# A style-modulated convolution kernel: both pairs of a quad in one product, four products in one PSUM region

## The chip, the cores and the metric

The kernel runs on one core of a Trainium2 chip. The metric is the device time of one launch in microseconds (us); lower is better.

## What is computed

128 samples of 64 channels and 1024 positions go through four 1-D convolutions of three taps (same, up by two with a blur, same, blur with down by two), and the result is added to the input. Each sample has its own weights:

```python
def _layer(x, style, w, b, mw, mb, typ):
    s = style @ mw.T + mb
    weight = SCALE * w * s[:, None, :, None]
    demod = lax.rsqrt(jnp.sum(weight * weight, axis=(2, 3)) + EPS)
    weight = weight * demod[:, :, None, None]
    ...                     # convolution of this type, then + b
x = x + L0(x, cond_512, ...)    # layers 'same', 'upsample', 'same', 'downsample'
```

Nothing nonlinear lies between the layers, so away from the ends of a row the four layers are one convolution of nine taps whose weights differ by sample. The kernel computes those nine weights for each sample (64x64 matrices) and convolves once. The six columns at the ends are computed layer by layer, for all samples together.

## The kernel before

**Units.** Two samples make a *pair* `p`: one sample in partitions 0 to 63, one in 64 to 127. Two pairs make a *quad* `q`; there are 32. TensorE works as four 64x64 quadrants, two row halves by two column halves, each with its own stream, so four matmuls run side by side. All data are fp32, and each fp32 matmul of the program is two records of LDWEIGHTS and MATMUL in the trace.

**Weights.** Stages 1 to 3 (`stage1` L362, `stage2` L393, `stage3` L430) build a quad's nine taps by matmuls into PSUM units `psS`, `psR`, `psW`; ScalarE evicts each with a scale per sample (`scaled_copy` L340) into `wd`, `S`, `R`, `Wf`. `stage3` runs in two parts. `combine` (L468 to L473, with `residual` L460) makes three sums of taps, the tile `H`, on VectorE. One PSUM buffer serves all these units in turn, `psE` of the ends too.

**Convolution.** The nine taps are done as three triples, in a scheme that needs five products instead of nine: each product is three matmuls over shifted columns. The input row lies in three interleaved planes. For a pair, `pre1` and `pre2` turn the planes `X` into five inputs, the five slots of a tile `T`, by way of a tile `G`: `G` by VectorE (L499, L504), slots 2 and 3 by GpSimd (`rest`, L510 and L511; for the first pairs VectorE), slot 4 by VectorE (L522), slots 0 and 1 by VectorE (L532). `SLOT` says which product reads which slot: products 0 and 4 read slots 0 and 1, products 1, 2 and 3 read slots 2, 3 and 4. `product` (L550) issues 12 matmuls of 170 columns; the two column halves of TensorE hold the two halves of a row's columns. `convA12` and `convA3` put products 1, 2 and 3 into three regions of one PSUM tile `psA`. ScalarE copies one of them (`copy_m1`, L573), `seed1` and `seed2` (L585) combine them on VectorE into `y1` and into two regions of the PSUM tile `Y`, and `convB` adds products 0 and 4 on top of `Y`. `output` (L642) scales and adds a bias on ScalarE, `store` (L647) sends half a pair, `load` (L132) fetches a pair.

**Order.** The order on each engine is the order of the program text (`manual_schedule`). The main loop runs over quads. In iteration q, with `c = q + 2` and `s = q + 3`, TensorE does: stage 2 of c, convB of the quad's first pair, stage 3 part 0 of c, products 1 and 2 of the next quad's first pair, stage 3 part 1, product 3, convB of the second pair, stage 1 of s, products 1 to 3 of the next quad's second pair. In some iterations `slot` adds a matmul group for the ends (`psE`, L792) and `extra` adds VectorE work for them. A prologue prepares quads 0 to 2.

**Buffers.** Tiles come from pools; a pool holds `bufs` buffers for each tag. Waits between engines are set by the framework from who writes and reads which tile. Before, `T` has four buffers of one pair each, and pair p+4 takes that of pair p: `pre1(p + 4)` stands behind `convB(p)` in the text.

## Time and profile before

| | |
|---|---|
| device time, three runs | 496.41, 496.79, 497.35 us (median 496.79) |
| the profiled execution | span 494.6 us; its own device time is not listed apart, the median lies 2.2 us above the span |
| instructions in the span | 28356 |
| GpSimd | busy 137.9 us (28%) |
| DMA | 70.81 MB, mean 143 GB/s |
| TensorE's granted clock, mean over the span | 0.998 |

The span runs from the first to the last instruction of the core. An engine's busy time says how much of the span it worked, not whether the work set the end. The chain follows the end back: at each step to what released an instruction, or to the one before it on the engine. In the tables of groups, a row is a line, engine and operation, `out<-in`, shapes, and a count; behind the bar stand busy us and mean ns of one. Matmul records are the latency of one and overlap.

### The profile page before, as it was taken

How to read it: one execution, taken by the hardware profiler on the slowest of the kernel's cores; microseconds unless marked ns; L12 is line 12 of the kernel's file. 1: busy time of each engine (PE TensorE's matmuls, PEld its weight loads, DVE VectorE, ACT ScalarE, POOL GpSimd, SP SyncE). 2: the span in 40 equal slices, each digit the busy share in tenths (PEclk: the TensorE clock that was granted, in tenths of full speed). 3: DMA queues.
4: the chain of work that ended last, by engine and by line, in shares of the span. 5: the costliest groups of instructions: out<-in, count | busy, mean ns of one | idle time of the engine just before them, and what ended most of it. 6: DMA issues, size and time to landing. Idle time of an engine off the chain costs nothing.

```text
span 494.6 us, 28356 instructions
## 1 busy us (share of the span) xinstructions
PE 485.9 (98%) x12600; PEld 475.6 (96%) x12600; DVE 442.4 (89%) x926; ACT 325.3 (66%) x797; POOL 137.9 (28%) x198
## 2 busy tenths in 40 slices
PE   8999999999999999999999999999999999999995
PEld 6899999999999999999999999999999999999995
DVE  5898989999999989988889998879999989988995
ACT  5566766766866657757667767657667667767652
POOL 3253234353322212212212222212222212222210
PEclk9999999999999999999999999999999999999999
DMA  8132654335544425553535554425544436544323
GB/s 255 50 98 89 216 168 150 108 115 174 173 157 148 153 67 175 173 173 115 139 99 173 168 165 147 144 76 173 163 147 155 135 99 191 173 160 130 97 109 129
DMA packets 37610, 70.81 MB, mean 143 GB/s; under 512 B 4208, under 2 KB 29040, under 8 KB 37488
## 3 DMA queue, kind: packets, MB, share of 16 engines
q1 hardware_dynamic: 37408, 68.88, 44.4%
q8 instruction: 99, 1.62, 1.4%
q14 instruction: 23, 0.19, 0.1%
q10 hardware_dynamic: 80, 0.11, 0.1%
HBM read 35.36 MB, written 33.62 MB: 139 GB/s over the span
## 4 chain that ended last, share of the span: by engine, by line
PE 96%; ACT 2%; DVE 1%; issue 0%; ACTq 0%; DVEq 0%
PE psA L550 32%; PE Y L550 22%; PE psR L393 17%; PE psW L430 14%; PE psS L362 7%; PE psE L792 2%; PE Y L173 1%; PE Y L316 1%; ACT Wf L340 0%; ACT m L573 0%; ACT R L340 0%; ACT ssq L206 0%; ACT sc L206 0%; PE psM L192 0%; DVE Y L585 0%
## 5 line engine op out<-in xcount | busy, mean ns | idle before, releaser
L550 PE MATMUL psA<-T,H 64*64 64x170 f32 x4608 | 205.4, 304 | 0.6 <-ACT m L573 0.6
L550 PEld LDWEIGHTS psA<-T,H 64*64 64x64 f32 x4608 | 188.4, 133 | 1.4 <-POOL o L644 0.9
L510 POOL TENSOR_TENSOR T<-G 128x342 f32<-128x342 f32 x62 | 57.9, 934 | 317.6 <-DVE G L504 194.8
L550 PE MATMUL Y<-T,Wf 64*64 64x170 f32 x3072 | 139.8, 304 | 1.4 <-ACT m L573 1.4
L550 PEld LDWEIGHTS Y<-T,Wf 64*64 64x64 f32 x3072 | 127.2, 133 | 2.6 <-ACT m L573 2.0
L642 ACT ACTIVATE o<-Y,oc,dm 128x340 f32<-128x340 f32 x125 | 79.5, 636 | 56.4 <-PE Y L550 56.1
L430 PE MATMUL psW<-R,par 64*64 64x256 f32 (+3 forms) x1536 | 98.7, 349 | 0.0
L393 PE MATMUL psR<-S,E 64*64 64x192 f32 (+1 forms) x2304 | 93.3, 299 | 0.1
L585 DVE SCALAR_TENSOR_TENSOR Y<-psA,u 128x340 f32<-128x340 f32 (+1 forms) x132 | 66.4, 507 | 30.1 <-ACT o L642 27.7
L340 ACT ACTIVATE Wf<-psW,t 128x256 f32<-128x256 f32 (+1 forms) x252 | 75.3, 381 | 22.6 <-PE psW L430 22.2
L430 PEld LDWEIGHTS psW<-R,par 64*64 64x64 f32 x1536 | 85.4, 133 | 2.5
L393 PEld LDWEIGHTS psR<-S,E 64*64 64x64 f32 x2304 | 85.9, 133 | 0.6 <-ACT S L340 0.2
L340 ACT ACTIVATE R<-psR,tC 128x448 f32<-128x448 f32 x63 | 36.5, 630 | 57.2 <-PE psR L393 57.2
L642 ACT ACTIVATE o<-y,oc,dm 128x170 f32<-128x170 f32 x125 | 65.7, 526 | 0.0
L499 DVE SCALAR_TENSOR_TENSOR G<-X 128x688 f32<-128x688 f32 x64 | 56.0, 874 | 4.6
L511 POOL TENSOR_TENSOR T<-G 128x342 f32<-128x342 f32 x62 | 57.2, 922 | 0.0
L532 DVE TENSOR_TENSOR T<-G 128x684 f32<-128x684 f32 x64 | 55.7, 871 | 0.0
L362 PE MATMUL psS<-wd,par 64*64 64x192 f32 x768 | 44.9, 329 | 0.0
L362 PEld LDWEIGHTS psS<-wd,par 64*64 64x64 f32 x768 | 37.0, 136 | 0.7 <-ACT raw L660 0.3
L573 ACT ACTIVATE m<-psA 128x340 f32<-128x340 f32 x64 | 29.2, 456 | 9.2 <-PE psA L550 6.4
L585 DVE SCALAR_TENSOR_TENSOR y<-psA,v 128x340 f32<-128x340 f32 x64 | 32.7, 512 | 2.2
L522 DVE TENSOR_TENSOR T<-X 128x342 f32<-128x342 f32 x64 | 33.6, 524 | 0.1
(131 smaller groups left out, 388.6 us busy)
## 6 DMA issues: line engine op xcount, KB each, us to landing
out<-o SPq DMA_DIRECT2D x126, 255.0 KB, 4.3
X<-in_x SPq DMA_DIRECT2D x60, 344.0 KB, 3.5
X<-in_x SPq DMA_DIRECT2D x60, 172.0 KB, 3.2
X<-in_x SPq DMA_DIRECT2D x4, 516.0 KB, 6.4
Xe<-in_x_ends SPq DMA_DIRECT2D x1, 512.0 KB, 5.8
par<-in_params SPq DMA_DIRECT2D x2, 192.0 KB, 3.5
out<-o SPq DMA_DIRECT2D x2, 170.0 KB, 2.8
par_s<-in_params_s SPq DMA_DIRECT2D x1, 196.0 KB, 2.8
```

The lines of the kernel that those rows point to most:

```text
L340: nc_a.activation(dst, src, AF.Copy, scale=f)
L362: nc.tensor.matmul(ps[r][cols, k * C : (k + K) * C], woi[2][rows, k, :], src[rows, :], start=(k == 0), stop=(k == K - 1), skip_group_check ...
L393: nc.tensor.matmul(ps[r][cols, lo * C : (lo + m) * C], E[rows, e + 2, :], src[rows, a, :], start=(n == 0), stop=(n == 8), skip_group_check ...
L430: nc.tensor.matmul(ps[r][cols, (lo - t_lo) * C : (hi - t_lo) * C], woi[0][rows, k, :], rt[c][rows, lo - k : hi - k, :], start=(k == order[0]),
L499: nc_v.scalar_tensor_tensor(g[:, PL:], X[:, : 2 * PL], 0.5, X[:, PL:], op0=ALU.mult, op1=ALU.subtract)
L510: eng.tensor_add(t[:, 2, :NJ], plane(g, 2), plane(g, 1))
L511: eng.tensor_sub(t[:, 3, :NJ], plane(g, 2), plane(g, 1))
L522: eng.tensor_sub(t[:, 4, :NJ], plane(X, 3), plane(X, 1))
L532: nc_v.tensor_sub(t[:, 0:2, :NJ], both(a, PL), both(b, 1))
L550: nc.tensor.matmul(ps[s][cols], w, Ts[p][rows, SLOT[m], j : j + NB], start=(g == 0 and m not in (0, 4)), stop=(g == 2), skip_group_check=True,
L585: nc_v.scalar_tensor_tensor(out, x, f, y, op0=ALU.mult, op1=ALU.add)
L642: nc_a.activation(dst, src, AF.Identity, bias=add, scale=d3)
```

## The change

**Both pairs in one product.** `X`, `G`, `T`, `o` and the sums hold a quad. The two column halves of TensorE take the two pairs, not two halves of the columns, so a matmul has 340 columns and a product of a quad is 12 matmuls, where it was 24. `T` has two buffers, each of a quad; `G`, `m3` and `y1` have one. `t_tile` makes `T` and `G` of a quad at its first use, which in the loop is `in3(c)`.

**Four products in one region.** For a quad, product 3 starts a region of the PSUM tile `A`; ScalarE copies it (`copy_m3`); product 1 is added on top; VectorE reads the sum (`sum1`); product 2 is added; VectorE reads again (`sum2`: it seeds `Y` and finishes `y1`); product 0 is added on top, and the region is the output of one plane. Product 4 goes into `Y`. Constant factors move into the weights.

**Stage 3 by kind of tap.** The nine taps lie as three kinds by three groups. Part 0 does kinds 0 and 1, part 1 kind 2, each from weights scaled beforehand (`scaled_weights`, on GpSimd); there are 9 steps of 192 and 128 columns, where there were 6 of 128 to 320. An eviction is one instruction, where it was two. `combine` is split into `combine_a` and `combine_b`.

**The loop.** The order in an iteration is new, with `n = q + 1`. A quad is stored in two DMAs, where it was four. The host changes the layout of the output.

The diff, cut; lines that are removed stand only where short:

```diff
-    tpool = ctx.enter_context(tc.tile_pool(name="tpool", bufs=4))
-    mpool = ctx.enter_context(tc.tile_pool(name="mpool", bufs=2))
-    gpool = ctx.enter_context(tc.tile_pool(name="gpool", bufs=2))
-    opool = ctx.enter_context(tc.tile_pool(name="opool", bufs=4))
+    tpool = ctx.enter_context(tc.tile_pool(name="tpool", bufs=2))
+    mpool = ctx.enter_context(tc.tile_pool(name="mpool", bufs=1))
+    gpool = ctx.enter_context(tc.tile_pool(name="gpool", bufs=1))
+    opool = ctx.enter_context(tc.tile_pool(name="opool", bufs=2))
...
-    NX = 4
+    NX = 2
     PL = NXC // 3
-    Xs = [const.tile([P, NXC], F32, name=f"X{i}") for i in range(NX)]
-    def load(p, planes=slice(0, 3)):
-        if p < NP:
+    Xs = [const.tile([P, 2, NXC], F32, name=f"X{i}") for i in range(NX)]
+    def load(q, planes=slice(0, 3)):
+        if q < NQ:
             at = slice(planes.start * PL, planes.stop * PL)
-            nc.sync.dma_start(Xs[p % NX][:, at], x[p, :, at])
+            for c in range(2):
+                nc.sync.dma_start(Xs[q % NX][:, c, at], x[2 * q + c, :, at])
...
+    w0s = [woi[0]] + [const.tile([P, K, C], F32, name=f"w0s{i}") for i in range(2)]
+    idn3 = const.tile([P, C], F32, name="idn3")
+    def scaled_weights():
+        for t, f in zip(w0s[1:], (1.0 / 3.0, -2.0)):
+            nc_g.tensor_scalar_mul(t, woi[0], f)
+        nc_g.tensor_scalar_mul(idn3, idn, 1.0 / 3.0)
...
+        kinds = ((0, 1), (2,))[part]
+        n = 0
+        for i, kind in enumerate(kinds):
+            for k in range(K):
+                gs = [g for g in range(K) if 0 <= K * g + kind - k < 7]
+                lo, m = gs[0], len(gs)
+                first = K * lo + kind - k
+                n += 1
+                for r, rows in enumerate(HALF):
+                    for c, cols in enumerate(HALF):
+                        at = (K * i + lo) * C
+                        nc.tensor.matmul(
+                            ps[r][cols, at : at + m * C],
+                            w0s[kind][rows, k, :],
+                            rt[c][rows, first : first + K * (m - 1) + 1 : K, :],
+                            start=(n == 1),
+                            stop=(n == K * len(kinds)),
+                            skip_group_check=True,
+                        )
+        for r in range(2):
+            dst = W[:, r, kinds[0] : kinds[-1] + 1].rearrange("c t g o -> c (t g o)")
+            scaled_copy(engs[r], dst, ps[r][:, : len(kinds) * K * C], t0[:, q, r : r + 1])
+        return ps
...
+    def residual(q):
+        W = Wq[q][0]
+        for r in range(2):
+            v = W[:, r, 1, 1, :]
+            nc_v.scalar_tensor_tensor(v, idn3, t3[:, q, r : r + 1], v, op0=ALU.mult, op1=ALU.add)
+    def sum_of(out, x, f, y, op=ALU.add):
+        nc_v.scalar_tensor_tensor(out, x, f, y, op0=ALU.mult, op1=op)
+    def taps(q):
+        W, H_ = Wq[q]
+        return *(W[:, :, i] for i in range(K)), *(H_[:, i] for i in range(3))
+    def combine_a(q):
+        chain.pop(q)
+        a, b, c, h1, h2, h3 = taps(q)
+        sum_of(h1, c, -2.0, a)
+        residual(q)
+        sum_of(h3, h1, 1.0 / 6.0, b)
+    def combine_b(q):
+        a, b, c, h1, h2, h3 = taps(q)
+        sum_of(h2, c, -0.5, a)
+        sum_of(h1, b, -3.0, h2, ALU.subtract)
+        sum_of(h2, h2, -1.0 / 3.0, b)
...
+    NJ = NB + 2
+    Ts = {}
+    Gs = {}
+    A = {}
+    SLOT = {0: 0, 4: 1, 1: 2, 2: 3, 3: 4}
...
+    def t_tile(q):
+        if q not in Ts:
+            Ts[q] = tpool.tile([P, 2, 5, PL], F32, tag="T", name=f"T{q}")
+            Gs[q] = gpool.tile([P, 2, 3 * PL], F32, tag="G", name=f"G{q}")
+        return Xs[q % NX], Ts[q], Gs[q]
+    def in3(q, pairs=BOTH_PAIRS):
+        if q < NQ:
+            X, t, g = t_tile(q)
+            nc_v.tensor_sub(t[:, pairs, 4, :NJ], plane(X, 3, pairs), plane(X, 1, pairs))
+    def in_g01(q, c):
+        if q < NQ:
+            X, t, g = t_tile(q)
+            sum_of(g[:, c, PL:], X[:, c, : 2 * PL], 0.5, X[:, c, PL:], ALU.subtract)
+    def in_g2(q, pairs=BOTH_PAIRS):
+        if q < NQ:
+            X, t, g = t_tile(q)
+            sum_of(plane(g, 2, pairs), plane(X, 3, pairs), 0.5, plane(X, 2, pairs), ALU.subtract)
+    def in1(q, eng):
+        if q < NQ:
+            X, t, g = t_tile(q)
+            eng.tensor_add(t[:, :, 2, :NJ], plane(g, 2), plane(g, 1))
...
+    def in04(q, c):
+        if q < NQ:
+            X, t, g = t_tile(q)
+            a, b = g[:, c, :NJ], g[:, c, 2 * PL : 2 * PL + NJ]
+            both = lambda v, step: bass.AP(v.tensor, v.offset, [list(v.ap[0]), [step, 2], [1, NJ]])
+            nc_v.tensor_sub(t[:, c, 0:2, :NJ], both(a, PL), both(b, 1))
+    def product(q, m, ps, groups=range(K)):
+        W, H_ = Wq[q]
+        for g in groups:
+            for s, rows in enumerate(HALF):
                 for c, cols in enumerate(HALF):
+                    if m in (0, 4):
+                        w = W[rows, c, m // 2, g, :]
+                    else:
+                        w = H_[rows, m - 1, c, g, :]
                     nc.tensor.matmul(
+                        ps[cols, s, :NB],
+                        w,
+                        Ts[q][rows, c, SLOT[m], g : g + NB],
+                        start=(g == 0 and m == 3),
+                        stop=(g == K - 1),
                         skip_group_check=True,
                     )
...
+    def conv3(q):
+        A[q] = ps_conv.tile([P, 2, 512], F32, tag="u", name=f"psA{q}")
+        product(q, 3, A[q])
+    def copy_m3(q):
+        m3c[q] = m_tile("m3", q)
+        nc_a.copy(m3c[q], A[q][:, :, :NB])
+    def conv1(q):
+        product(q, 1, A[q])
+    def sum1(q):
+        y1w[q] = m_tile("y1", q)
+        sum_of(y1w[q], A[q][:, :, :NB], 2.0, m3c[q])
+    def conv2(q):
+        product(q, 2, A[q])
+    def sum2(q):
+        a = A[q][:, :, :NB]
+        sum_of(Y[:, :, :NB], m3c.pop(q), 3.0, a)
+        nc_v.tensor_sub(y1w[q], y1w[q], a)
+    def conv4(q):
+        product(q, 4, Y)
+    def conv0(q, *groups):
+        product(q, 0, A[q], groups)
...
+    def output(q, i, s, eng=nc_a):
+        if q not in os:
+            os[q] = opool.tile([P, 2, K, NB], F32, tag="o", name=f"o{q}")
...
+        src = (A[q][:, s, :NB], y1w[q][:, s], Y[:, s, :NB])[i]
...
+    def store(q, s, planes=slice(0, K)):
+        nc.sync.dma_start(
+            out[q, :, s, planes.start * NB : planes.stop * NB],
+            os[q][:, s, planes].rearrange("c i j -> c (i j)"),
+        )
...
     stage3(0, 0, None, BOTH)
     stage3(0, 1, ps_conv, BOTH)
     stage1(1, ps_conv)
     stage1(2)
+    combine_a(0)
+    combine_b(0)
     const_rest(0, PART[0], const_of(0, PART[0]))
+    in2(0, nc_v)
     stage2(1, ps_conv)
+    conv3(0)
+    copy_m3(0)
     const_first(1, PART[0])
+    in04(0, 0)
+    in04(0, 1)
...
+    conv1(0)
...
+    sum1(0)
...
+    stage3(1, 1)
+    mod_by_layer(LATER, raw[0][:, 0], ssq, AF.Square)
+    in_g01(1, 0)
     scale3(3)
+    conv2(0)
...
     EXTRA = {
+        (0, 0): lambda: (
+            var_inverse(PART[1]),
+            var_newton(PART[1]),
+            table_A(PART[1], dm[:, 2, PART[1]]),
+            [of(PART[1]) for of in (table_C, vector_c0, table_3, vector_Da)],
+        ),
...
+        n, c, s = q + 1, q + 2, q + 3
         if q == 1:
             nc.sync.dma_start(Xe, x_ends)
         if q == 5:
             zeros()
         if c < NQ:
             stage2(c)
+        if q == 0:
+            var_matmul(PART[1], var_of(PART[1]), start=False)
+            var_root(PART[1], var_of(PART[1]))
+        sum2(q)
+        if n == NQ - 1:
+            conv3(n)
+            copy_m3(n)
+            conv4(q)
+            for i in range(2):
+                output(q, 2, i)
+            combine_b(n)
+            in04(n, 0)
+            in04(n, 1)
+            conv1(n)
+            for i in range(2):
+                output(q, 1, i)
+            sum1(n)
+            conv0(q, 0, 1)
+            conv2(n)
+            conv0(q, 2)
+            for i, eng in enumerate(BOTH):
+                output(q, 0, i, eng)
+                store(q, i)
+            continue
+        if q == 0:
+            combine_a(1)
+        if n < NQ:
+            combine_b(n)
+        conv4(q)
+        for i in range(2):
+            output(q, 2, i)
+        if n == NQ:
+            for i, eng in enumerate(BOTH):
+                output(q, 1, i, eng)
+            for i in range(2):
+                store(q, i, slice(1, 3))
+            conv0(q, *range(K))
+            for i, eng in enumerate(BOTH):
+                output(q, 0, i, eng)
+                store(q, i, slice(0, 1))
+            break
         if c < NQ:
             stage3(c, 0)
+        conv3(n)
+        copy_m3(n)
+        if q == 0:
+            in_g01(1, 1)
+            in_g2(1)
+            load(n + NX)
+            in1(1, nc_g)
+            in2(1, nc_g)
+        in04(n, 0)
+        in04(n, 1)
+        in3(c)
         if c < NQ:
             stage3(c, 1)
+        conv0(q, 0, 1)
+        if q in SLOTS:
+            slot(*SLOTS[q])
+        conv1(n)
+        for i in range(2):
+            output(q, 1, i)
+        for i in range(2):
+            in_g01(c, i)
+        in_g2(c)
+        load(c + NX)
+        in1(c, nc_g)
+        in2(c, nc_g)
+        extra(q, 0)
+        sum1(n)
         extra(q, 1)
+        conv0(q, 2)
+        output(q, 0, 0)
         if s < NQ:
             stage1(s)
+        output(q, 0, 1)
         if s + 1 < NQ:
             scale3(s + 1)
+        conv2(n)
         if c < NQ:
+            combine_a(c)
+        for i in range(2):
+            store(q, i)
```

## The prediction

> **What bounds the kernel now.** First the page: busy shares and the chain that ended last.

> ```profile
> PE 485.9 (98%) x12600; PEld 475.6 (96%) x12600; DVE 442.4 (89%) x926; ACT 325.3 (66%) x797; POOL 137.9 (28%) x198
> ...
> PE 96%; ACT 2%; DVE 1%; issue 0%; ACTq 0%; DVEq 0%
> ```

> TensorE (PE) carries 96% of the chain. Whether it streams at its limit is read from the chain in order of time and from matmul groups by shape (columns of the chain: start us, us, what).

> ```profile
> 256.04 0.08 PE psR L393
> ...
> 268.13 2.31 PE psA L550 x64
> ...
> 270.44 0.07 PE psR L393
> ```

> ```profile
> L430 PE MATMUL psW<-R,par 64*64 64x320 f32 x256 | 30.4, 430 | 0.0
> ...
> L393 PE MATMUL psR<-S,E 64*64 64x128 f32 x1024 | 70.4, 269 | 0.0
> ```

> From 320 to 128 columns a matmul gets shorter by 161 ns: 0.839 ns a column. The 64 records of 170 columns took 2.31 us, 16 in each quadrant: 144.4 ns, of which 142.6 are columns and 2 a fixed cost. Stage 2 to stage 2 is one quad: 14.40 us. The columns of a quad per quadrant are 60 x 170 (conv), 6 x 192 (stage 1), 10 x 192 and 8 x 128 (stage 2), 2688 (stage 3): 16,984, or 14.25 us, and 96 records by 2 ns make 14.44. So PE streams without a gap, and only columns, records or a new wait can move the time. Waits on PE are few: 0.98 us at 99.0, 1.03 at 114.3, 0.90 at 480.3.

> Then what a change of buffers can do: who waited for the T tiles (waits: us in total, times, longest), and one such place in the timeline.

> ```profile
> POOL T L510 <- PE Y L550: 46.8, 10, 7.0
> ```

> ```profile
> 250.73 0.51 DVE L504 SCALAR_TENSOR_TENSOR G<-X 128x342 f32<-128x342 f32 x1
> ...
> 251.51 0.96 PE L550 MATMUL Y<-T,Wf 64*64 64x170 f32 x18
> ...
> 252.89 0.91 POOL L510 TENSOR_TENSOR T<-G 128x342 f32<-128x342 f32 x1 [5.84 <-PE Y L550]
> ```

> This is iteration 14. GpSimd writes slot 2 of T[33] into the buffer of T[29]. Slot 2 of T[29] was read by product 1, in a psA run whose last record ended at 240.5, and its input G was ready at 251.24; yet it starts at 252.89, 0.14 us after the last of convB(29) (252.45 + 0.30), which reads slots 0 and 1. So the new tile waits for the last reader of the whole old tile, not of its slot.

> **The change, part by part**, each against the profiled execution (span 494.6; the median is 2.2 above it).

> *Stream.* Columns stay. Conv records per quadrant go from 60 to 30, stage 3 from 12 to 18: 24 fewer by 2 ns, 0.05 us a quad, -1.5 us in all. [...] In the new text a product takes 6 x 287 = 1.72 us, stage 1 0.98, stage 2 2.50, stage 3 1.53 and 0.77: 14.38 a quad.

> *VectorE, ScalarE, GpSimd.* VectorE has ten sums of 340 less a quad and three of 680 more; ScalarE four evictions and a copy less; GpSimd two operations of 684 for four of 342. All of it lies beside PE. These engines had 11%, 34% and 72% of the span free, so I cost it at nothing. GpSimd takes `scaled_weights` in the prologue and drops `table_02` (four operations to two); it waits there anyway.

> *Reads between products.* Product 3 to product 1: `copy_m3`, 0.46 us at 340 columns (L573), some 0.74 at 680, behind two evictions; PE has stage 3 part 1 and two thirds of product 0 between, 1.9 us. `sum2` to product 4: 0.88 us under stage 2's 2.50. Product 1 to 2: `sum1`, 0.88 (below), under a third of product 0 and stage 1, 1.55. Covered, as long as VectorE comes to them in time; uncovered, about 1 us a quad each.

> *The new wait.* It doesn't stay in time. `T` has two buffers; while iteration q runs, T[q] and T[n] hold them. `in3(c)`, the first write of T[c], stands on VectorE ahead of `in_g01`, `in_g2`, `extra(q, 0)` and `sum1(n)`. By the 252.89 row it must wait until the last reader of T[q] is through, and that is now `conv0(q, 2)`, behind product 1 in PE's order. `sum1(n)` sits behind it, and PE's product 2 waits for `sum1(n)`. So every iteration holds a ring: conv0(q, 2) ends; then `in3`, `in_g01` twice, `in_g2`, `sum1`; then product 2. Its price is from these rows:

> ```profile
> L499 DVE SCALAR_TENSOR_TENSOR G<-X 128x688 f32<-128x688 f32 x64 | 56.0, 874 | 4.6
> L532 DVE TENSOR_TENSOR T<-G 128x684 f32<-128x684 f32 x64 | 55.7, 871 | 0.0
> ```

> ```profile
> 243.79 0.88 DVE L499 SCALAR_TENSOR_TENSOR G<-X 128x688 f32<-128x688 f32 x1
> ...
> 244.59 0.51 DVE L504 SCALAR_TENSOR_TENSOR G<-X 128x342 f32<-128x342 f32 x1
> ```

> Back to back, the next starts 0.80 us after an 0.88 us start. All five are this wide (684, 688, 688, 684, 680): 4 x 0.80 + 0.88 = 4.08, and 0.14 from PE to the first: 4.2 us. Only stage 1 (0.98) runs beside it. PE stands still 3.2 us in each of the 30 iterations with a quad c: +97 us (bounds 2.9 to 3.6: 87 to 108). What was queued before `in3` (sum2, combine_b, in04: 5 us) has passed by then, so the 5 us in which VectorE is idle ahead of `in3` help nobody.

> *Extras.* What `extra(q, 0)` puts on VectorE now lies in the ring in full, where it lay beside PE. From the rows: reciprocals 2 x 0.66, Newton steps 1.9, table_A 0.4, setup_x 2 x 0.6, setup0 and setup3 0.9, rest0 0.95, setup1 0.6, rest1_bias 2 x 1.05, rest2 1.25, three blur sides 1.8, rest3_bias 1.05: 13.5; in iteration 0 another 1.6. +15 us (10 to 18).

> *Start and tail.* In iteration 0 `sum2(0)` stands behind `var_root`, which needs matmuls after stage 2 and a ScalarE operation that queues behind two evictions of 0.63: product 4 waits some 2.4 us. Product 1 waits for GpSimd's `in1(1)`, 0.8. The new prologue has the same matmuls. +3 (0 to 6). In the tail `sum2(31)` stands behind a VectorE output of 0.63: +1 (0 to 3). The three waits of before go: -2.7.

> Sum: -1.5 + 97 + 15 + 3 + 1 - 2.7 = +112: span 606.6, device time 608.8. SP's loads wait for `in_g2(c)`, and a quad's load has more than an iteration before it is used; stores are two for four of the same bytes.

> *The clock.* PE's gap has a second price. The windows (start:end, length, busy of each engine with counts, then granted clock, DMA share, GB/s) at the end of the run:

> ```profile
> 491.00:492.00 1.00, 0.00 (x0) 0.00 (x0) 0.00 (x0) 0.00 (x0) 0.00 (x0) 1.00 0.95 312
> 492.00:493.00 1.00, 0.00 (x0) 0.00 (x0) 0.00 (x0) 0.00 (x0) 0.00 (x0) 0.65 0.49 167
> 493.00:494.00 1.00, 0.00 (x0) 0.00 (x0) 0.00 (x0) 0.00 (x0) 0.00 (x0) 0.50 0.00 0
> ```

> The last matmul ended at 489.55; 0.65 over the window from 492 means a fall to one half at 492.3, 2.75 us later. Gaps of 1 us (99.0, 114.3) brought no fall. A gap of 3.2 us, more with extras, is in reach of it. How long the clock then stays down no row shows; at the start PE is busy from 5.6 us on, and stage 1's matmuls still come in 2.19 us at 8.5, where they later take 0.98, so some 5 us at half rate, 2.5 us lost, is an upper end. Bounds: 0 to 30 x 2.5 = 75 us. The gap is only 0.45 us above the 2.75 seen, so I take half of the iterations and three quarters of the price: 15 x 1.9 = 28 us. Forecast 637.

> [...]

> **The rivals.** *No ring:* the buffer is handed on once those readers are through that stand ahead of `in3(c)` in the text. Then VectorE has all five done by the time product 1 ends, the covers above hold, and the sum is -1.5 - 2.7 + 3 + 1 = 0: 496.8 (492 to 500). For it: in the 252.89 row convB(29) also stood ahead in the text, so the row alone does not tell the two apart. Against it: `conv0(q)` still needs what lies in that buffer, and the 252.89 wait shows no slots kept apart. It decides at one point: whether `in3(c)` starts before conv0(q, 2) ends. 9%; the one case that is not slower. *Ring, clock stays full:* 609 (596 to 618): 24%; for it, 3.2 us may be too short. *Ring, clock falls nearly every time:* 609 + 60 to 75, 668 to 684: 17%. *The forecast, ring and some falls:* 618 to 668, 45%. The remaining 5% lies between 500 and 596 or above 684, if the five operations cost less in their new shapes or a second wait joins.

> **How the numbers follow.** 637 is the likeliest case's middle. The range 598 to 672 holds that case, most of the full-clock case and the low end of the many-falls case: 45 + 22 + 12 of 100. About 0.2% (1 us) can be told from no change. The no-ring case lies around no change: faster 0.05, same 0.02, slower with its rest and all others 0.93.

> **What would show it.** Right: one L-row of `in3` (T<-X, 128x684) with idle time on VectorE released by PE psA, about 5 us each, 30 times; PE's idle time before product 2 released by VectorE's `y1` sum, about 3.2 us; stage 2 to stage 2 some 17.6 us at full clock; granted clock under 1 in many slices, mean 0.85 to 0.97. Wrong: stage 2 to stage 2 at 14.4 (no ring); PE busy share near 98%; a gap before product 2 and a mean clock at 1.0 (no falls); gaps at product 1 or product 4 (a read not covered).

## The result, and the profile after

The changed kernel takes 695.22 us (median of four runs, 691.92 to 697.14) against 496.99 us before: ratio 1.398, 95% interval 1.395 to 1.402. The forecast was 637 with a range from 598 to 672: the direction was right, the size too small. It lies above the 684 of the case with many falls too, where the prediction had left a small part of 5%. The profiled execution has a span of 695.3 us, 200.7 more than before, and a mean granted clock of 0.904.

The page first: busy shares, the granted clock in 40 slices, the chain that ended last.

```profile
PE 540.5 (78%) x9520; PEld 381.4 (55%) x9520; DVE 435.6 (63%) x632; ACT 288.4 (41%) x578; POOL 132.1 (19%) x142
...
PEclk9997999989899889899999889999899999899988
...
PE 68%; DVE 25%; issue 4%; DMA 1%; ACT 1%; SPq 0%; DVEq 0%; ACTq 0%
```

TensorE went from 98% busy to 78%, VectorE from 89% to 63%: both stand, in turn, and a quarter of the chain is now VectorE's. The clock falls below full in slices all through the loop. The waits (us in total, times, longest) name the pair:

```profile
DVE T L494 <- PE psA L533: 201.8, 30, 9.5
...
PE psA L533 <- DVE y L451: 138.7, 32, 7.4
```

30 times VectorE's `in3(c)` (L494) waits for a product in `psA`, and 32 times TensorE, ahead of a product in `psA`, waits for VectorE's sum `y1` (L451). One iteration (14) in the chain in order of time (start us, us, what):

```profile
355.82 0.02 issue
355.84 0.04 DVE T L494
355.88 0.75 issue
356.63 2.44 DVE G L451 x3
359.07 0.79 DVE y L451
359.85 0.14 issue
359.99 3.44 PE psA L533 x24
```

This is the ring that the prediction drew: `conv0(q, 2)` ends, then `in3`, three `G`, `sum1`, then product 2. From `in3` to product 2 it takes 4.15 us (forecast 4.2), and TensorE, with stage 1 beside it, stands 3.23 us (forecast 3.2). The last line is what comes on top: product 2 takes 3.44 us (the granted clock is 0.50 from 360.28 to 363.70), where the same 24 records take 1.95 after such a stop at full clock (the chain of `vector_busy` below). In other iterations the ring itself is longer: up to 8.3 us, 42.8 us in all above 30 times its shortest. Where this comes from is shown by one operation of the ends, a sum on 64 partitions, in the view of one source line (min/median/max ns, first and last start). After:

```profile
L799 DVE SCALAR_TENSOR_TENSOR Ue<-b1s,Ue x4: 1573/1593/1611, 379.3 to 404.7; 64x64 f32<-64x64 f32 x4
```

The same operation before:

```profile
L843 DVE SCALAR_TENSOR_TENSOR Ue<-b1s,Ue x4: 269/271/273, 265.2 to 279.9; 64x64 f32<-64x64 f32 x4
```

Nothing in it was changed, and it takes six times as long. In the timeline of the changed kernel GpSimd's `in1` and `in2` (L509, L514) run beside it, because they start when `G` is done, and `G` is done inside the ring:

```profile
378.72 1.98 POOL L509 TENSOR_TENSOR T<-G 128x684 f32<-128x684 f32 x1 [16.06 <-DVE G L451]
380.66 1.66 POOL L514 TENSOR_TENSOR T<-G 128x684 f32<-128x684 f32 x1
```

The chain of the same iteration (15) has the first two of the four sums:

```profile
379.25 1.57 DVE Ue L799
...
380.84 1.61 DVE Ue L799
```

Each ends about when the GpSimd operation beside it ends (380.70 and 382.32). Other rows of this trace show the same beside `in1` or `in2`: a sum `H` (L451, 128x384) took 0.55 us alone (median) and up to 1.99, a sum `Wf` (L448) 0.27 and up to 1.67, a copy of one input (`a`, L741) 0.18 and 1.61. From 60 us on, 57 operations of VectorE with all inputs in SBUF started while `in1` or `in2` ran, 0.15 us or more before its end, and each ended 0.03 to 0.62 us after it; ten ended while it ran, a reciprocal (0.75 us) and nine `sum1`, with one input in PSUM (0.81 to 0.87 us, 0.87 alone).

### The profile page after: what moved, and what is told of

It reads as the page before. It is cut to its first block, busy times and chain, and to the rows that moved or that the text cites. A ratio compares the mean times of both kernels' runs of the same rounds, so it can differ in the third digit from the quotient of the medians.

```text
span 695.3 us, 20952 instructions
## 1 busy us (share of the span) xinstructions
PE 540.5 (78%) x9520; PEld 381.4 (55%) x9520; DVE 435.6 (63%) x632; ACT 288.4 (41%) x578; POOL 132.1 (19%) x142
## 4 chain that ended last, share of the span: by engine, by line
PE 68%; DVE 25%; issue 4%; DMA 1%; ACT 1%; SPq 0%; DVEq 0%; ACTq 0%
PE psA L533 36%; PE psR L389 11%; PE psW L430 11%; DVE G L451 10%; PE Y L533 9%; DVE y L451 4%; DVE H L451 1%; PE psE L748 1%; DVE Wf L448 1%; DVE Ue L799 1%; DMA X<-in_x 1%; DVE Y L451 1%; DVE nw L237 1%; DVE Ve L764 1%; ACT o L587 1%
## 5 line engine op out<-in xcount | busy, mean ns | idle before, releaser
L533 PE MATMUL psA<-T,H 64*64 64x340 f32 x2304 | 221.4, 519 | 139.5 <-DVE y L451 138.7
L533 PEld LDWEIGHTS psA<-T,H 64*64 64x64 f32 x2304 | 103.4, 150 | 214.9 <-issue 143.9
L494 DVE TENSOR_TENSOR T<-X 128x684 f32<-128x684 f32 (+1 forms) x33 | 28.2, 854 | 201.8 <-PE psA L533 201.8
L509 POOL TENSOR_TENSOR T<-G 128x684 f32<-128x684 f32 x31 | 54.0, 1743 | 511.2 <-DVE G L451 511.2
L451 DVE SCALAR_TENSOR_TENSOR G<-X 128x688 f32<-128x688 f32 (+1 forms) x97 | 78.2, 860 | 0.7 <-DMA X<-in_x 0.7
L533 PE MATMUL Y<-T,Wf 64*64 64x340 f32 x768 | 64.0, 463 | 6.5 <-DVE Y L451 6.3
L533 PE MATMUL psA<-T,Wf 64*64 64x340 f32 x768 | 67.6, 447 | 0.0
L336 ACT ACTIVATE Wf<-psW,t 128x384 f32<-128x384 f32 (+1 forms) x126 | 56.3, 497 | 12.5 <-PE psW L430 12.5
L430 PE MATMUL psW<-R,w0s 64*64 64x128 f32 (+1 forms) x1536 | 61.3, 287 | 0.0
L514 POOL TENSOR_TENSOR T<-G 128x684 f32<-128x684 f32 x31 | 57.2, 1846 | 0.0
L430 PEld LDWEIGHTS psW<-R,w0s 64*64 64x64 f32 x1536 | 50.6, 133 | 7.6
L587 ACT ACTIVATE o<-Y,tb,td 128x340 f32<-128x340 f32 x64 | 37.1, 630 | 32.2 <-ACT R L336 17.1
L451 DVE SCALAR_TENSOR_TENSOR H<-Wf 128x384 f32<-128x384 f32 x64 | 46.8, 731 | 0.0
L533 PEld LDWEIGHTS Y<-T,Wf 64*64 64x64 f32 x768 | 31.4, 137 | 26.2 <-DVE Y L451 6.1
L451 DVE SCALAR_TENSOR_TENSOR Y<-m,psA 128x680 f32<-128x680 f32 x32 | 27.7, 866 | 21.1 <-PE psA L533 21.1
```

Of the source, the lines that this page charges most:

```text
L336: nc_a.activation(dst, src, AF.Copy, scale=f)
L430: nc.tensor.matmul(ps[r][cols, at : at + m * C], w0s[kind][rows, k, :], rt[c][rows, first : first + K * (m - 1) + 1 : K, :], start=(n == 1 ...
L451: nc_v.scalar_tensor_tensor(out, x, f, y, op0=ALU.mult, op1=op)
L494: nc_v.tensor_sub(t[:, pairs, 4, :NJ], plane(X, 3, pairs), plane(X, 1, pairs))
L509: eng.tensor_add(t[:, :, 2, :NJ], plane(g, 2), plane(g, 1))
L514: eng.tensor_sub(t[:, :, 3, :NJ], plane(g, 2), plane(g, 1))
```

## The experiments

The theory: the third quad's `T` tile waits for the last reader of the buffer's old quad, and so makes the ring; on top come the extras in it, VectorE slowed by GpSimd, and the clock. Its rivals: the loss belongs to the reads between the products, or to the order, or to VectorE's load.

### A third buffer: `three_t`

```diff
-    tpool = ctx.enter_context(tc.tile_pool(name="tpool", bufs=2))
+    tpool = ctx.enter_context(tc.tile_pool(name="tpool", bufs=3))
```

> Changed kernel with three buffers for T instead of two; nothing else. Ring theory (in3(c) waits for the last reader of T[q], and product 2 waits behind it): the third buffer frees in3, so no idle time ahead of it, stage 2 to stage 2 at 14.4 to 14.6 us, granted clock 0.99 or more, 492 to 508 us. Rival (the reads between the four products of one region hold TensorE, whatever the buffers do): still above 640 us, with the same 3.2 us ahead of product 2.

513.54 us, ratio 1.032 (1.030 to 1.035). One number took away 182 of the 198 us. The wait of L494 is gone, the mean clock is 0.986, and in iterations without extras stage 2 to stage 2 takes 14.33 us, 0.06 below the 14.39 of before. So the four products in one region, the reads between them and stage 3 by kind cost these iterations nothing; with extras, TensorE waits 0.4 to 1.4 us for `sum1` in four. But 513.5 is over the expected bound of 508: 16.6 us stay. Of the span, iteration 0 takes 26.89 us (before 14.39), iterations 1 to 28 take 417.0 (before 416.2), and from the last stage 2 to the end it is 37.2 (before 32.7). The chain in iteration 0:

```profile
50.12 1.30 DVE nw L236
...
51.44 1.56 DVE nw L237
...
53.65 0.88 DVE y L451
...
54.66 3.68 PE psA L533 x24
```

The Newton step of samples 16 to 31, beside GpSimd's `in1` and `in2`, stands ahead of `sum1(1)`; product 2 waits 6.1 us for it, and then takes 3.68 us, at half clock.

### The same buffers, `in3` later: `in3_late`

`in3(c)`, from behind `in04`, and the load of X, from behind `G`, move to behind `sum1(n)`; two buffers stay.

```diff
-        in3(c)
...
-        load(c + NX)
...
         sum1(n)
+        in3(c)
+        load(c + NX)
         extra(q, 1)
```

> Changed kernel with two buffers for T; in3(c), and the load that must follow it, stand behind sum1(n) in the text. Ring theory: in3 then waits where nobody waits for it, under 1 us, and the time is that of three buffers within 8 us (492 to 512). Rival (space or the wait of the whole tile costs wherever it stands, since GpSimd's two inputs and the next loads come later): above 540.

567.07 us, ratio 1.142 (1.139 to 1.144): the expected 492 to 512 was missed, and the time is in the rival's range. The wait before product 2 goes, and 128 us with it, so the ring is one of order as much as of buffers. A new wait comes; the waits of this kernel:

```profile
POOL T L509 <- PE psA L533: 357.7, 29, 14.8
...
PE Y L533 <- DVE Y L451: 47.2, 30, 2.8
```

GpSimd's `in1(c)` may now start when `conv0(q, 2)` ends, and so it runs beside `in3` and `combine_a(c)`, which stand ahead of `sum2(n)`; product 4 waits for `sum2` 30 times. Whether VectorE is late by its own work or by GpSimd's is the question of `late_vector` below.

### GpSimd taken out: `on_vector` and `late_vector`

```diff
         in04(n, 0)
         in04(n, 1)
+        if q:
+            in1(n, nc_v)
+            in2(n, nc_v)
...
-        in1(c, nc_g)
-        in2(c, nc_g)
```

`on_vector` does this to the changed kernel, so the ring stays; `late_vector` does it to `in3_late`.

> Changed kernel, ring kept; the inputs of products 1 and 2 (in1, in2) go from GpSimd to VectorE, behind in04 of the next iteration, where VectorE sits idle. Theory of a shared path (VectorE operations with two SBUF inputs stand still while a GpSimd operation reads SBUF): rest1_bias's and setup0's small copies go back from 1.59 and 0.91 us to 0.3 or less, residual from 0.45 to 0.28, extras in the ring from 36 to 14 us, 660 to 675 us. Rival (these operations are slow by their shapes or by the place): rows as in the changed kernel, 690 or more.

667.09 us, ratio 1.340 (1.334 to 1.346): 28.1 us less, though VectorE has 2 x 684 columns a quad more to do. The sum of L799 is back at its old time:

```profile
L799 DVE SCALAR_TENSOR_TENSOR Ue<-b1s,Ue x4: 265/268/271, 356.8 to 377.9; 64x64 f32<-64x64 f32 x4
```

What the rings take above their shortest falls from 42.8 to 16.9 us in all. So 26 of the 42.8 were VectorE's operations lengthened beside GpSimd, and 17 the extras themselves.

> Two T buffers, in3(c) and the load behind sum1 as in in3_late (567.1 us), and in1 and in2 on VectorE instead of GpSimd. Theory (what was left of in3_late's loss is VectorE slowed by GpSimd's in1 and in2, so that sum2 came late to product 4): 505 to 525 us, PE's wait for the Y sum before product 4 nearly gone. Rival (VectorE's own queue between sum1 and sum2 is too long, whoever works beside it): above 545 us, the wait stays 1.5 us an iteration or more.

514.30 us, ratio 1.033 (1.029 to 1.037), and product 4's waits for `sum2` are down to 4.6 us in all. With two buffers and no third, the kernel is where `three_t` is. What was left in `in3_late` was GpSimd beside VectorE, not VectorE's queue.

### The clock: `busy_pe`, `vector_busy`, `half_fill`

TensorE multiplies zeros into `Y` while it waits for product 2; two sets take 0.57 us (an estimate: 680 columns in each quadrant at the 0.839 ns that the rows of before gave), and `FILL` gives each iteration as many pairs of sets as its wait asks for (5 by default).

```diff
+        if c < NQ:
+            zeros_to_y(2 * FILL.get(q, 5), NB)
         conv2(n)
```

> Changed kernel, ring kept; ahead of product 2 TensorE gets matmuls of zeros into Y (which nobody reads then), 2.9 us in most iterations, 4.6 to 6.9 where extras stand in the ring. Clock theory (the falls of the clock after the gaps cost some 50 us): granted clock 0.98 or more, 640 to 655 us. Rival (the half clock falls on time in which TensorE is idle and costs little): clock near 1, but 685 or more.

665.45 us, ratio 1.339 (1.337 to 1.341), mean clock 0.989. The wait is as long as before and only filled, and 29.8 us go: less than the theory asked for, more than its rival. With the clock full, `sum2` comes late to product 4, which the falls had mostly hidden: start and tail apart, TensorE waits for it in ten iterations, 0.35 to 1.34 us each and 8.2 in all, where the changed kernel has two such waits, 1.8.

`vector_busy` joins it with `on_vector`, so that the ring stands alone.

> The ring stays (two T buffers, in3 where the change put it), but in1 and in2 run on VectorE and TensorE multiplies zeros into Y while it waits for product 2. So the ring's wait is left without the two things that came on top of it: VectorE slowed by GpSimd, and the fallen clock. Theory (the wait costs about 3.2 us an iteration, the rest of the loss was those two): 612 to 630 us, mean clock above 0.98, from the 608.8 of the sum before the clock, and 8 to 15 us for the start and late sums. Rival (TensorE is late for another reason, the falls only hid it): above 645 us, with a period of 19 us or more in most iterations.

627.27 us, ratio 1.263 (1.259 to 1.266), mean clock 0.991. In four iterations without extras stage 2 to stage 2 takes 17.71 us; forecast was 17.6. One ring of it in the chain:

```profile
541.67 0.87 DVE T L494
542.54 2.35 DVE G L451 x3
544.90 0.79 DVE y L451
...
545.73 1.95 PE psA L533 x24
```

`half_fill` leaves out six sets in each iteration, so that TensorE stands some 2.0 us, not 3.2.

```diff
-            zeros_to_y(2 * FILL.get(q, 5), NB)
+            zeros_to_y(2 * (FILL.get(q, 5) - 3), NB)
```

In the trace of the changed kernel the 26 falls of the clock from 30 us on begin whole multiples of 3.413 us apart (the first at 39.43 us, the last at 684.55, 189 multiples later).

> vector_busy (627.3 us) with six sets of zeros less in every iteration: TensorE again stands idle, but about 2.0 us ahead of product 2 and not 3.2. Theory (the clock falls only when TensorE is idle for most of one 3.4-us window, as the 2.75 us at the end of the run before suggest): no falls in the loop, clock above 0.98, 624 to 632 us. Rival (an idle share of about half a window is enough): falls in many iterations, clock under 0.95, 645 us or more.

654.21 us, ratio 1.315 (1.309 to 1.321): the rival was right. Two stretches of windows show why (start:end, length, busy of PE, PEld, DVE, ACT, POOL with counts, granted clock, DMA share, GB/s):

```profile
247.22:250.63 3.41, 1.49 (x26) 0.49 (x18) 3.38 (x6) 1.38 (x4) 0.00 (x0) 1.00 0.31 51
250.63:254.04 3.41, 3.41 (x76) 2.55 (x80) 3.34 (x8) 0.00 (x0) 0.00 (x0) 1.00 0.95 253
267.70:271.11 3.41, 1.31 (x20) 0.51 (x16) 3.37 (x8) 0.98 (x3) 0.00 (x0) 1.00 0.40 82
271.11:274.52 3.41, 3.41 (x40) 2.14 (x36) 1.80 (x3) 0.00 (x0) 0.00 (x0) 0.50 0.92 287
```

These windows lie on that grid of 3.41 us. In the first TensorE is idle 1.92 us (56%), and the clock stays at 1.00; in the third 2.10 us (62%), and the whole next window is at 0.50. Over the changed kernel and six of the experiments (`three_t`, `in3_late`, `on_vector`, `busy_pe`, `vector_busy`, `half_fill`), from 30 us on, each window at full clock in which TensorE was idle 60% or more was followed by one at half (78 of 78), and none of the 32 with 45 to 56%; of the 19 in between, 10 were. The changed kernel alone has 26 of 26 with 65% or more and none of 13 with 45 to 59%. Not the longer gap brought the fall, but the larger share of one window: in the changed kernel a gap of 3.76 us (546.12 to 549.88) lay half in each of two windows, 55% idle both, and the clock stayed at 1.00; one of 2.20 us (36.46 to 38.66) lay in one, 65% idle, and the next was at 0.50. The price follows too: `half_fill` has 54.6 us more of TensorE's work at half clock than `vector_busy`, which lose half, 27.3; the spans differ by 24.8 and the medians by 26.9.

### The start and the tail: `three_t_start`, `three_t_vec`

```diff
     in_g01(1, 0)
+    in_g01(1, 1)
+    in_g2(1)
+    load(1 + NX)
+    in1(1, nc_g)
+    in2(1, nc_g)
...
-        (0, 0): lambda: (
-            var_inverse(PART[1]),
+        (0, 1): lambda: (
+            var_root(PART[1], var_of(PART[1])),
+            var_inverse(PART[1]),
```

These stand on `three_t`; what is added in the prologue and in `extra(0, 1)` goes from iteration 0's old places.

> Three T buffers, and VectorE's and GpSimd's work of iteration 0 taken apart: G, in1 and in2 of quad 1 move to the end of the prologue; var_root, the inverse, Newton and table of samples 16 to 31 move behind sum1. Theory (16.6 us of three_t over before are the start: iteration 0 is held by VectorE's queue): iteration 0 falls from 26.9 to 15 to 17 us, 500 to 506 us in all. Rival (the work is only moved, and iteration 1 or 2 takes the time): 509 us or more.

502.17 us, ratio 1.010 (1.007 to 1.014). Iteration 0 falls from 26.89 to 15.95 us, and 11.4 of the 16.6 us are gone. The tail (37.1 us) is as it was: product 4 of the last quad waits 2.3 us for `sum2(31)`, which stands behind an output on VectorE, and then takes 3.33 us at half clock.

> three_t_start with in1 and in2 on VectorE in the loop. Theory (beside a product that TensorE streams without a gap, GpSimd's slowing of VectorE costs little): within 3 us of three_t_start. [...] Rival 2 (VectorE, with 13 us of work in 14.4, becomes the bound in the iterations with extras): 4 us or more above three_t_start.

501.88 us, ratio 1.010 (1.006 to 1.013): by the time the theory's case, no difference from `three_t_start`. But the profiled executions show two differences that cancel: iterations 1 to 28 take 413.3 us, where `three_t_start` has 416.7, and the tail takes 40.1, where it has 37.1, with a second window at half clock (mean clock 0.990, where it has 0.996). So outside the ring GpSimd's slowing of VectorE still costs the loop some 3 us; that the two times come out equal is luck.

### What the change is worth without its waits: `best_vec`, `best_gp`, `best_two`

`best_vec` joins three buffers, `in1` and `in2` on VectorE, the start, and a new order of the last products:

```diff
+        if q < NQ - 1:
+            sum2(q)
...
             conv3(n)
             copy_m3(n)
-            conv4(q)
...
+            conv0(q, 0)
...
             conv1(n)
             sum1(n)
-            conv0(q, 0, 1)
+            conv4(q)
...
             conv2(n)
-            conv0(q, 2)
+            sum2(n)
+            conv0(q, 1, 2)
```

> Three T buffers; in1 and in2 on VectorE in the loop (GpSimd for the last quad); the start as in three_t_start, with the samples-16-to-31 matmul behind stage 3 part 0 and var_root and inverse ahead of sum1; in the last three iterations thirds of product 0 moved into the waits, and sum2 of the last quad ahead of the outputs. Theory (after the ring only the start, the tail and VectorE's slowing are left, and TensorE's stream is 0.06 us a quad shorter than before): 493 to 497.5 us, at or below before (496.8). Rival (a new wait in the reordered tail, or VectorE late in the iterations with extras): 499 us or more.

> best_vec with in1 and in2 left on GpSimd. Theory: sum1 comes 0.3 to 1.4 us late in iterations 4, 6, 15 and 16 as in three_t_start, so 2 to 4 us above best_vec: 496 to 500. Rival (those waits are hidden again): within 1 us of best_vec.

> best_vec with the change's own two T buffers: in3(c) and the load behind sum1 instead of a third buffer. Theory (the place of in3 does what the third buffer does, once GpSimd is out of VectorE's way): within 4 us of best_vec, 494 to 501. Rival (in iterations with extras sum2 comes late because in3, G and extras all lie between sum1 and sum2): 503 us or more.

`best_vec`: 497.19 us, ratio 1.0014 (1.0002 to 1.0027), no difference beyond the 0.2% that can be told. `best_gp`: 498.22, ratio 1.0034 (1.0022 to 1.0047), 1.0 above `best_vec`, between its two cases: the loop is 2.4 us longer, the tail 1.0 shorter. `best_two`: 504.39, ratio 1.0166 (1.0144 to 1.0187), by the time its rival's case, 7.2 us above `best_vec`; but the rival's cause is only about half of it. Iterations 1 to 28 take 3.6 us more, most of it in four with extras (7, 16, 23 and 24). The tail takes 4.2 more: the last quad's `in1` and `in2`, which all three versions leave to GpSimd, run here beside `combine_a`: a sum that takes 0.55 us elsewhere takes 2.00, a pair of 0.47 takes 1.84, and product 3 waits 3.5 us. The page of `best_vec`:

```profile
PE 483.1 (98%) x9520; PEld 369.6 (75%) x9520; DVE 414.1 (84%) x690; ACT 288.8 (58%) x578; POOL 32.7 (7%) x84
...
PE 93%; DVE 4%; ACT 1%; DMA 1%; issue 1%; DVEq 0%; ACTq 0%
```

TensorE is at 98% again. Iterations 1 to 28 take 414.6 us against 416.2; iteration 0 is still 1.2 us longer and the tail 1.1. The change removes a quarter of TensorE's records (9520 for 12600), and all that it gains in these iterations is 1.6 us, 0.06 an iteration, as the prediction's *Stream* estimated. No version ran faster than the kernel before.

## Why the prediction fell short, point by point

The experiments make a ladder between the two kernels, each rung below the first one cause (medians, us; the interplay of two causes goes to the rung that is taken later):

| rung | step | measured | forecast |
|---|---|---|---|
| before to `three_t` | all but the ring: stream, old waits, start, tail | +16.6 | -0.2 |
| `three_t` to `vector_busy` | the ring and the extras in it | +113.7 | +112 |
| `vector_busy` to `on_vector` | the clock | +39.8 | +28 |
| `on_vector` to the changed kernel | VectorE beside GpSimd | +28.1 | 0 |

- *The new wait* and *extras*: right, in cause and size. The reading of one row, that a new tile waits for the last reader of the whole old tile, also holds for a reader that stands later in the text; this was the step that the rival of no ring denied. `in3` waited 201.8 us over 30 places (6.7 us each, forecast about 5). The extras themselves took 17 us (15).
- *VectorE, ScalarE, GpSimd*: "I cost it at nothing" is the step that failed most: of the 58 us between 637 and 695.2 it is 28.1, start, tail and old waits 16.8, the clock 11.8, the ring 1.7. The shares of idle time were right, but they say nothing of what two engines do to one another. The ring moved GpSimd's `in1` and `in2` to the moment at which VectorE is the path, and the extras were priced by rows that had no such neighbour: 28 us. Outside the ring the same slowing costs the loop 2.4 to 3.4 us (`best_gp` against `best_vec`, `three_t_start` against `three_t_vec`). With the clock full it also delays `sum2`: in iterations 26 and 28 of the changed kernel, where the clock stays up until product 4, `combine_a` is slowed (a sum `H` 1.47 us and the two `Wf` 1.79, where `three_t_start` has 0.55 and 0.47), and the chain goes through it, if only just (stage 2 ends at 615.49, product 4 starts at 615.57). The chain of iteration 26:

```profile
610.12 0.77 DVE y L451
610.90 1.47 DVE H L451
612.36 1.79 DVE Wf L448 x2
...
615.57 1.95 PE Y L533 x24
```

- *The clock*: mechanism right, size off. The 2.75 us at the end of the run before was read as the idle time that a fall needs, and half of the iterations as its odds. It was only the distance from the last matmul to the end of a window: in the trace of before, the clock's rise at 11.03 us and its fall at 492.31 lie 141 x 3.413 us apart. By an estimate from these numbers a gap of 3.23 us puts the 2.0 us into one window in most positions: it fails only where the window's end lies in its middle 0.7 us (2 x 1.98 - 3.23), 0.7 / 3.41 or one time in five. The changed kernel has 12 gaps of 3.15 to 3.25 us from 30 us on, and 4 brought no fall. It had 26 falls from there on, and in 11 of them, with TensorE idle 24% or more of the window at half, a second followed. Its records show 104 us of TensorE's work at half clock, where half is lost, and `busy_pe` 11.2: 46 us of difference. Of these 33.3 came back between the two spans (29.8 between the medians). 6.4 of the rest are the waits for `sum2` that the falls had hidden; what remains isn't divided.
- *Start and tail*: 4 us were set, 16.6 and more were needed. Of the two waits named the first was there (2.2 us ahead of product 4, forecast 2.4), the second (0.8 at product 1) was not. What was left out or priced too low lies behind them: in iteration 0 VectorE has five `G` where others have three, and the Newton steps, 1.3 and 1.6 us beside GpSimd where they take 0.22 each alone (`before`), all ahead of `sum1(1)`. In the tail `sum2(31)` was priced by its own delay and not by the product at half clock that follows it (3.33 us in `three_t_start`). The three waits of before are 2.9 us by the prediction's own rows (0.98, 1.03, 0.90), not the 2.7 of its sum, which changes nothing.
- *The rivals*: the case of a ring with falls nearly every time (668 to 684) is close to what `on_vector` shows, 667.1: GpSimd's part is what no case held.
- *Stream*: right. 24 records of 340 columns take 1.715 us (forecast 1.72), and an iteration of `three_t` without extras is 0.06 us shorter than before, which the prediction gave as 0.05.
- *Reads between products*: covered, as forecast, where VectorE has no extras: with `three_t`'s period at 14.33 none of them shows. With extras `sum1` is late in four iterations of `three_t`, 2.6 us in all.
- The signs of being right that it named were all seen: the row of `in3`, 3.23 us before product 2, 17.71 us a quad with the clock full, a mean clock of 0.904 (0.85 to 0.97).

What stays open: the rungs are one order of taking the causes away, and their interplay (the late `sum2` that the falls hide) isn't divided further; taken in the other order, by way of `busy_pe`, the clock is 29.8 and GpSimd's part 38.2. Where the 2.2 us come from that iterations 0 and 1 of `best_vec` still take above before is open.

## What to carry to other kernels

When buffers are merged into fewer and wider ones, follow for each new tile the last reader of the old one, in the order of every engine, and see what is queued behind the first write: a wait there holds up all that follows it. Moving that write behind the sum that the other engine needs, or one more buffer, was worth 128 and 182 us here; the quarter of TensorE's records that the change saves brought 0.06 us an iteration. Then price everything that the wait brings together in time anew: an operation off the path that now runs beside the path's engine, and idle time of TensorE by how much of it falls into one window of the clock, 3.41 us here.
